# Attention scores from float32r halves of queries and keys, moved to their rows by DMA, and GraphSAGE's bias product over 128 rows

## The chip, the cores and the metric

The kernel runs on one core of one Trainium2 chip, in one launch. The core has five engines that run side by side, each in the order of its own program: TensorE (PE, with its weight loads shown as PEld), VectorE (DVE), ScalarE (ACT), GpSimd (POOL) and SyncE (SP), which here only issues transfers. They meet through semaphores. Sixteen DMA engines carry the transfers that SP, ACT and POOL issue. The metric is the device time of one execution in microseconds (us).

## The reference

Two graph layers over 16 graphs of 1024 nodes with 128 features. Each layer normalises its input, applies ReLU, computes, and adds the result to its input.

```python
# layer 0: attention over the edges, 8 heads of 16
h = relu(layernorm(x))
q, k, v = h @ Wq.T + bq, h @ Wk.T + bk, h @ Wv.T + bv        # split into heads
scores = q @ k.T / sqrt(16);  scores[adj == 0] = -inf
attn = softmax(scores) * adj;  attn = attn / (attn.sum(-1) + 1e-8)
x = x + (attn @ v) @ Wo.T + bo
# layer 1: dilated neighbours, then three GraphSAGE layers
h = relu(layernorm(x));  adj_d = adj * dilate(adj > 0)         # row by row, sequential
for i in 1..3:
    out = (adj_d @ h / max(sum(adj_d), 1)) @ Wr_i + h @ Wx_i + b_i
    h = h_i = batchnorm(relu(out / norm(out)))
x = x + concat(h_1, h_2, h_3) @ Wl + bl
```

`dilate` walks the 1024 rows of each graph and removes every n-th neighbour of a row, in both directions; it needs the adjacency alone.

## The kernel before

**First stage: attention, with the dilation beside it.** The attention loop (`attention`, L471) runs over 256 turns `(b, c, m)`: graph b, half c of the 512 query nodes, tile m of 128 key nodes. A turn has two half-turns, one for each head group g: heads 2j + g, j = 0 to 3. In a half-turn

- `scores` (L530) puts -1e30 where there is no edge, with sixteen small bf16 products over 32x32 strips (L545), and adds the scores with four products (L551), one head each, on the four 32-row strips of the array;
- ScalarE takes exponentials in two pieces of 1024 columns (L589), VectorE multiplies each by the transposed adjacency tile `aT` (L594);
- PE adds the values product and the 1e-8 term of the half-turn before (`values`, L475, lines L478 and L483).

The query and key projections give 128 rows, 16 to a head, so each 32-row strip holds two neighbouring heads, one of either group. `key` (L311) writes them to SBUF as they are (`kT`, L316). `query` (L302) writes two copies (L307), in each of which the rows of the other group are multiplied by zero through the column `own`. So a product over 32 rows gives one head's scores. Operands are float32.

`turn_over` (L488), two turns ahead, transposes the adjacency tile on PE (L496), stores it to HBM as `aT_d` for the second stage (L500), makes the no-edge mask, and has SP shift that mask to other partitions with six transfers (L507, L508). `load` fetches adjacency tiles three turns ahead.

Everything else of the attention, the preparation of the next graph (`prepare`, L284: layer norm, transposes, key, value and query projections of either half) and the conclusion of the last one (`conclude`, L379: division, output projection, layer norm for the next layer), is written as generators. The loop takes one step of them at fixed places of a half-turn (`go_on_with`, L461): "True" steps, which need a PSUM bank, in the second half-turn of a turn, and "evict" steps, which empty that bank, after the exponentials and multiplications of the same half-turn.

The dilation (`dilation`, L642) is VectorE work, with ScalarE and PE helping. It goes through 8 blocks of 128 rows, for all graphs at once: seven counting rounds in small steps (L829 and the lines around), then a sweep over the 16 graphs' whole rows (L892 to L924), which stores removed edges to HBM (`mr_d`). `beside_attention` (L935) feeds its steps in after each half-turn, in proportion to planned costs, so that the dilation ends just before the attention does. The sweep's row tiles `wr` and `er` have rings of their own; the rounds use a ring of four buffers named `mr`.

**Second stage: GraphSAGE.** Three layers, 16 graphs, two halves: 96 turns. A turn (`nodes`, L1091) begins with the bias, a product of a 3-row matrix of ones with the bias split into three bf16 pieces (`start_with`, L108, L111), adds the node's own term (L1102), sums the neighbours in four groups of products (L1116), and ends in normalisation on VectorE. `edges` (L128) loads 2 MB of adjacency (L132) and two mask tiles (L136) for a turn, three turns ahead, into buffers `aT0` to `aT3`; the third of these buffers holds the attention's value rows `v1_both` until the attention is over. VectorE applies the masks (L145). Between the stages the conclusion of the last half graph runs inside the first GraphSAGE turns.

**Order.** In both stages the programs of PE, ScalarE and VectorE run in the order in which the Python code emits them. SP and POOL also issue in order: an issue that waits for its data holds back those behind it.

Of the kernel before, what the change touches and what calls it, by code (L numbers as in the profile page):

```python
# [10 lines left out]
F32 = mybir.dt.float32  # L11
BF = mybir.dt.bfloat16
# [9 lines left out]
P = 128  # L22
# [12 lines left out]
def swept(ctx: ExitStack, tc: tile.TileContext, t: dict, out: bass.AP, flag: bass.AP):  # L35
# [11 lines left out]
    H = 8  # L47
# [34 lines left out]

    ones3 = const.tile([3, P], BF, name="ones3")
    nc.vector.memset(ones3, 1.0)
# [3 lines left out]
    bias3 = const.tile([3, len(names), D], BF, name="bias3")  # L88
# [19 lines left out]
    def start_with(ps_tile, pieces):  # L108

        n = ps_tile.shape[1]  # L110
        nc.tensor.matmul(  # L111
            ps_tile.rearrange("p k d -> p (k d)"), ones3, pieces.unsqueeze(1).to_broadcast([3, n, D]),
            start=True, stop=False,
        )
# [51 lines left out]
    def first_part(p1):  # L166
# [33 lines left out]
        raw = pool.tile([P, 4, D], F32, name="raw", tag="kT")  # L200
        for i, name in enumerate(names):
# [3 lines left out]
        bk = one.tile([P, 1], F32, name="bk")  # L205
        nc.sync.dma_start(bk, t["L0_gnn_bk"].rearrange("(d o) -> d o", o=1))

        own = one.tile([P, 2], F32, name="own")
        nc.vector.tensor_reduce(
            own,  # L210
            ident.rearrange("p (j g d) -> p g j d", g=2, d=HD),
            AX.XY,
            ALU.add,
        )
        bq = one.tile([P, 3], F32, name="bq")
        nc.sync.dma_start(bq[:, 2:3], t["L0_gnn_bq"].rearrange("(d o) -> d o", o=1))
# [3 lines left out]
        def turn_weights():  # L220
            wps = ps_d.tile([P, 4, D], F32, name="wps", tag="d")
            for i in range(4):
                nc.tensor.transpose(wps[:, i, :], raw[:, i, :], ident)
            yield
            nc.vector.tensor_copy(attn_w, wps)
            nc.vector.tensor_tensor(bq[:, 0:2], own, bq[:, 2:3].to_broadcast([P, 2]), ALU.mult)
            yield
# [13 lines left out]
        v1_both = shared.tile([P, 2, NB, H, 32], F32, name="v1_both", tag="aT2")  # L241
        v1s = [v1_both[:, i] for i in range(2)]
        for v1 in v1s:
            nc.vector.memset(v1[:, :, :, HD:], 0.0)
            nc.vector.memset(v1[:, :, :, HD : HD + 1], 1.0)
# [38 lines left out]
        def prepare(b):  # L284
# [15 lines left out]
            kT = pool.tile([P, N], F32, name=f"kT_{b}", tag="kT")  # L300

            def query(c, bank=(ps_m, "m")):  # L302
# [3 lines left out]
                for g in range(2):  # L306
                    nc.scalar.activation(  # L307
                        qTs[c][:, g, :], pq, AF.Identity, bias=bq[:, g : g + 1], scale=own[:, g : g + 1]
                    )

            def key(c, bank=(ps_m, "m")):  # L311
# [4 lines left out]
                nc.scalar.activation(kT[:, cc], pk, AF.Identity, bias=bk)  # L316
# [3 lines left out]
            def value(c, bank=(ps_m, "m")):  # L320
                pv = bank[0].tile([P, HB, D], F32, name=f"pv_{b}_{c}", tag=bank[1])
                start_with(pv, bias3[:, 0, :])
                for i in range(HB):
# [6 lines left out]
                    v1[:, c * HB : (c + 1) * HB, :, :HD], pv.rearrange("p k (h d) -> p k h d", d=HD)  # L330
                )

            if b == 0:
# [14 lines left out]
                qTs = [pool.tile([P, 2, HN], F32, name=f"qT_{b}_0", tag="qT")]  # L348
                yield from query(0, (ps_d, "d"))
                yield from second  # L350
                ready[b] = (xt, qTs, kT, v1)
# [3 lines left out]
                yield from turned(1)  # L355
            else:
# [7 lines left out]

                yield "half 1"
                qTs = [pool.tile([P, 2, HN], F32, name=f"qT_{b}_0", tag="qT")]
                yield True
                yield from query(0)

            ready[b] = (xt, qTs, kT, v1)  # L370
            for what in (key, value):
                yield True
                yield from what(1)
            yield "half 0"
            qTs.append(pool.tile([P, 2, HN], F32, name=f"qT_{b}_1", tag="qT"))
            yield True
            yield from query(1)

        def conclude(b, c, acc, xt):  # L379

            yield False
            cx = small.tile([P, HB, H, HD], F32, name=f"cx_{b}_{c}", tag="cx", bufs=1)
# [30 lines left out]
            start_with(pr, bias3[:, 1, :])  # L413
# [31 lines left out]
        ready = {}  # L445

# [24 lines left out]
        def attention():  # L471
# [3 lines left out]
            def values(acc, v1, m, g, es, ws):  # L475

                for j in range(4):
                    nc.tensor.matmul(  # L478
                        acc[g][32 * j : 32 * j + 32, :], v1[:, m, 2 * j + g, :],
                        ws[j // 2][:, j % 2, :], start=(m == 0), stop=False,  # L480
                    )
# [48 lines left out]
            def scores(i, g):  # L530
# [4 lines left out]
                _, qTs, kT, _ = ready[b]  # L535
                nomask = tiles[i][1]
                mm = slice(m * P, (m + 1) * P)
# [11 lines left out]
                for j in range(4):  # L549
                    rows = slice(32 * j, 32 * j + 32)  # L550
                    nc.tensor.matmul(  # L551
                        scs[j // 2][:, j % 2, :], kT[rows, mm], qTs[c][rows, g, :],
                        start=False, stop=True, tile_position=(32 * j, 0),
                    )
# [3 lines left out]
            for i, (b, c, m) in enumerate(turns):  # L558
# [12 lines left out]
                for g in range(2):  # L571
# [32 lines left out]
                    go_on_with(False)  # L604
                    if i + g + 1 < len(turns):
# [36 lines left out]
        def dilation():  # L642
# [84 lines left out]
            for k in range(NB):  # L727
# [151 lines left out]
                wrs, gms, ers, ets = {}, {}, {}, {}  # L879
# [8 lines left out]
                for i in range(B + 2):  # L888
                    b = i
                    if b < B:  # L890
                        wrs[b] = pool.tile([P, N], F16, name=f"wr_{k}_{b}", tag="wr", bufs=2)
# [15 lines left out]
                    if 0 <= b < B:  # L907
                        er = ers[b] = pool.tile([P, N], BF, name=f"er_{k}_{b}", tag="er", bufs=3)
# [56 lines left out]
        def judge():  # L965
# [5 lines left out]
            fits = pool.tile([P, B * NB * H], F32, name="fits", tag="kT")  # L971
# [119 lines left out]
    def nodes(L, b, c, hT, aT):  # L1091
# [7 lines left out]
        start_with(own, bias3[:, 2 + L, :])  # L1099
# [859 lines left out]
```

## Time and profile before

| | |
|---|---|
| median of 3 runs | 3486.12 us (3484.86 to 3486.22) |
| the profiled execution | 3484.92 us |
| its span, first to last instruction | 3483.0 us |
| PE busy | 3389.0 us (97%) |
| VectorE busy | 3092.4 us (89%) |
| ScalarE busy | 2286.4 us (66%) |
| GpSimd busy | 174.4 us (5%) |
| last exponentials of the attention | 2353.6 us after the start |

Lines such as L551 are those of the kernel before. A group's row gives line, engine, operation, what it writes and reads, shape and number, then its busy time, the mean time of one in nanoseconds, and the idle time of the engine just before its instructions with what ended it. Busy time counts overlapping instructions once: four products that run together on four strips of the array are busy for as long as one, although each has its own mean. Matmul ends are modelled. In a table by stretches of time the columns are busy us (and instructions) of PE, PEld, DVE, ACT and POOL, the granted PE clock, the DMA share and GB/s.

### The profile page before, as it was taken

To read this page: it belongs to the slowest core of one execution; us is meant where nothing else is said; L and a number is where in the kernel's file an instruction comes from. 1 tells how busy PE (TensorE), PEld (TensorE's weight loads), DVE (VectorE), ACT (ScalarE), POOL (GpSimd) and SP (SyncE) were. 2 spreads that over 40 slices of the span, in tenths; PEclk is the share of its full clock that TensorE was granted. 3 is DMA by queue.
4 is the path that set the end of the run, shared out by engine and by line. 5 is a ranking of instruction groups with operands and counts; after the bars stand their busy time and mean duration, and the time that the engine had idled before them with its cause. 6 is when DMAs were issued, how large, how long until landed. Compare 5 with 4: busy or idle time off the path is not lost. (4 is left out here: it accounts for less than half of the span.)

```text
span 3483.0 us, 86073 instructions
## 1 busy us (share of the span) xinstructions
PE 3389.0 (97%) x34855; PEld 1877.8 (54%) x34855; DVE 3092.4 (89%) x5254; ACT 2286.4 (66%) x3781; POOL 174.4 (5%) x253
## 2 busy tenths in 40 slices
PE   8999999999999999999999999999999899999997
PEld 3333333333333333333333334338999899989997
DVE  7899999989989989999999998988788788878886
ACT  7699689789779869868977886873222333332224
POOL 2000000000000000000000000000000000000000
PEclk9999999999999999999999999999999999999999
DMA  7366456447547647736754864768999799989996
GB/s 239 108 175 197 131 158 195 150 140 218 171 130 219 190 125 208 231 113 186 229 157 141 243 199 128 218 190 314 330 333 325 270 328 326 335 309 332 332 333 215
DMA packets 650121, 772.27 MB, mean 222 GB/s; under 512 B 173264, under 2 KB 569168, under 8 KB 637424
## 3 DMA queue, kind: packets, MB, share of 16 engines
q1 hardware_dynamic: 632672, 708.58, 63.1%
q0 software_dynamic: 15456, 57.30, 5.0%
q8 instruction: 275, 4.51, 0.6%
q14 instruction: 134, 1.10, 0.1%
q10 hardware_dynamic: 1584, 0.79, 0.1%
HBM read 508.50 MB, written 157.29 MB: 191 GB/s over the span
## 5 line engine op out<-in xcount | busy, mean ns | idle before, releaser
L594 DVE TENSOR_TENSOR w<-e,aT 128x1024 f32<-128x1024 f32 x1024 | 1203.6, 1216 | 104.0 <-ACT e L589 103.4
L589 ACT ACTIVATE e<-sc 128x1024 f32<-128x1024 f32 x1024 | 990.5, 1020 | 341.9 <-PE sc L551 340.8
L1116 PE MATMUL pg<-y,aT 128*128 128x128 f32 (+1 forms) x6144 | 737.3, 275 | 0.0
L1116 PEld LDWEIGHTS pg<-y,aT 128*128 128x128 f32 x6144 | 711.7, 192 | 0.0
L478 PE MATMUL acc<-w,v_both 128*32 128x512 f32 x4096 | 636.4, 605 | 8.0 <-DVE w L594 4.9
L483 PE MATMUL acc<-e,eps 128*32 128x512 f32 x4096 | 617.2, 593 | 0.0
L551 PE MATMUL sc<-qT,kT 32*128 32x512 f32 x4096 | 584.0, 640 | 0.5 <-ACT qT L307 0.5
L145 DVE SCALAR_TENSOR_TENSOR aT<-mr,aT 128x1024 f32<-128x1024 bf16 x384 | 458.7, 1216 | 0.0
L483 PEld LDWEIGHTS acc<-e,eps 128*32 128x32 f32 x4096 | 159.0, 110 | 293.8 <-issue 284.9
L1139 ACT ACTIVATE sq<-o 128x512 f32<-128x512 f32 x96 | 60.6, 631 | 361.6 <-DVE o L1134 361.6
L892 DVE TENSOR_TENSOR_SCAN wr<-rk 128x1024 f16<-128x1024 bf16 x128 | 291.6, 2278 | 0.0
L545 PEld LDWEIGHTS <-never 32*32 32x32 bf16 x8192 | 78.4, 88 | 339.3 <-issue 317.3
L545 PE MATMUL sc<-nomask,never 32*32 32x512 bf16 x8192 | 246.5, 385 | 11.8 <-ACT e L589 6.7
L551 PEld LDWEIGHTS sc<-qT,kT 32*128 32x128 f32 x4096 | 160.0, 183 | 116.9 <-issue 116.1
L478 PEld LDWEIGHTS acc<-w,v_both 128*32 128x32 f32 x4096 | 100.6, 108 | 204.7 <-DVE w L594 105.8
L496 PEld LDWEIGHTS pa<-ident,a 128*128 128x128 f32 x1024 | 107.8, 141 | 181.6 <-issue 139.7
L1157 ACT COPY hT<-pt 128x512 f32<-128x512 f32 x96 | 56.2, 585 | 224.2 <-PE pt L1153 214.3
L1134 DVE SCALAR_TENSOR_TENSOR o<-pg,rdeg,mine 128x128 f32<-128x128 f32 x384 | 108.1, 344 | 88.9 <-PE pg L1116 87.1
L905 ACT ACTIVATE wr<-wr,th 128x1024 f16<-128x1024 f16 x128 | 148.0, 1156 | 46.7 <-DVE wr L892 45.7
L496 PE MATMUL pa<-ident,a 128*128 128x128 f32 x1024 | 168.4, 287 | 6.9 <-DMA a<-in_adj 6.2
L503 ACT ACTIVATE nomask<-aT 128x512 bf16<-128x512 f32 x256 | 161.3, 630 | 8.1
L499 ACT COPY aT<-pa 128x512 f32<-128x512 f32 x256 | 151.6, 592 | 5.3 <-PE pa L496 4.8
(225 smaller groups left out, 3840.7 us busy)
## 6 DMA issues: line engine op xcount, KB each, us to landing
aT<-aT_d SPq DMA_DIRECT2D x94, 2048.0 KB, 9.1
mr<-mr_d SPq DMA_DIRECT2D x188, 512.0 KB, 5.9
aT_d<-aT SPq DMA_DIRECT2D x256, 256.0 KB, 4.2
a<-in_adj SPq DMA_DIRECT2D x253, 256.0 KB, 4.1
ad<-in_adj SPq DMA_DIRECT2D x112, 512.0 KB, 4.2
nomask<-nomask SPq DMA_DIRECT2D x512, 96.0 KB, 2.7
nomask<-nomask SPq DMA_DIRECT2D x512, 64.0 KB, 2.7
nomask<-nomask SPq DMA_DIRECT2D x512, 32.0 KB, 2.8
```

Source lines behind the costliest of these rows:

```text
L145: nc.vector.scalar_tensor_tensor(part, mrs[h][:, j : j + 2, :].rearrange("p j n -> p (j n)"), 0.0, part, ALU.is_equal, ALU.mult)
L478: nc.tensor.matmul(acc[g][32 * j : 32 * j + 32, :], v1[:, m, 2 * j + g, :], ws[j // 2][:, j % 2, :], start=(m == 0), stop=False,)
L483: nc.tensor.matmul(acc[g][32 * j : 32 * j + 32, :], eps8, es[j // 2][:, j % 2, :], start=False, stop=(m == NB - 1),)
L496: nc.tensor.transpose(pa[:, k * P : (k + 1) * P], a[:, k, :], ident)
L499: nc.scalar.copy(aT[:, 0, :], pa)
L503: nc.scalar.activation(nomask[:, 0, :], aT[:, 0, :], AF.Relu, bias=1.0, scale=-1e38, accum_out=zeros[:, i : i + 1])
L545: nc.tensor.matmul(scs[j // 2][to : to + 32, j % 2, :], never[rows, rows], nomask[rows, j, :], start=True, stop=False, tile_position=(32 * ...
L551: nc.tensor.matmul(scs[j // 2][:, j % 2, :], kT[rows, mm], qTs[c][rows, g, :], start=False, stop=True, tile_position=(32 * j, 0),)
L589: nc.scalar.activation(e, scs[q], AF.Exp, scale=1.0 / math.sqrt(HD))
L594: nc.vector.tensor_tensor(w, es[q], aT.to_broadcast([P, 2, HN]), ALU.mult)
L892: nc.vector.tensor_tensor_scan(wrs[b], rk(b, 1, N + 1), rk(b, 2, N + 2), -1023.0, ALU.add, ALU.add)
L1116: nc.tensor.matmul(pg[:, i // 2, at : at + width], aT[:, j, i * P : (i + 1) * P], y[:, j, :width], start=(j == 0), stop=(j == NB - 1),)
```

## The change

**Scores.** A float32 score product becomes two float32r products. `halves` splits a projection as it leaves PSUM: ScalarE adds the bias and writes the result rounded to float32r, and VectorE writes what is left (product plus bias minus the rounded value), also as float32r. Both go to one buffer, `split_home`. The projection weights are turned with their columns in another order, so that heads of group 0 come first: head j of group g stands in rows 16(4g + j) on.

`move` then queues sixteen transfers from there to a tile that `scores` reads. Strip j has 32 rows: 16 for one half of the head's key, 16 for the other (`ks`, a tile for each half of the nodes, with one copy for each g). In the queries' tile (`qs`) both 16-row parts of a strip hold the same rows, once for each of the two halves. A product over 32 rows gives (key's first half + key's second half) times one half of the query; `scores` runs two of them, one for each half of the query, in groups of four strips. Transfers of group 0 go through POOL's queue, those of group 1 through SP's. `move_on(8)` at the end of a half-turn issues up to eight of those that are queued; for the first graph's first key and query `move_on(16)` issues all at once before the attention loop starts.

**Room.** The value rows take 17 columns a head instead of 32 in the same 16 KB (`both`), which now also holds `cx` of `conclude` and `split_home`. The sweep's `wr` and `er` become pairs in the `mr` ring. The biases of query and key come in with sixteen small loads. In graphs past the first the second half's value comes before its key.

**Bias.** The matrix of ones and the bias pieces have 128 rows, those past the third zero; GraphSAGE's products run over all 128, the attention's over three as before.

```diff
-    ones3 = const.tile([3, P], BF, name="ones3")
+    ones_bf = const.tile([P, P], BF, name="ones_bf")
...
-    bias3 = const.tile([3, len(names), D], BF, name="bias3")
+    bias3 = const.tile([P, len(names), D], BF, name="bias3")
+    nc.vector.memset(bias3, 0.0)
...
-    def start_with(ps_tile, pieces):
+    def start_with(ps_tile, i, rows=3):
         n = ps_tile.shape[1]
         nc.tensor.matmul(
-            ps_tile.rearrange("p k d -> p (k d)"), ones3, pieces.unsqueeze(1).to_broadcast([3, n, D]),
+            ps_tile.rearrange("p k d -> p (k d)"), ones_bf[:rows], bias3[:rows, i, :].unsqueeze(1).to_broadcast([rows, n, D]),
             start=True, stop=False,
         )
...
+        bqk = one.tile([P, 2], F32, name="bqk")
+        for i, name in enumerate(("L0_gnn_bq", "L0_gnn_bk")):
+            by_g = t[name].rearrange("(j g d o) -> g j d o", g=2, d=HD, o=1)
+            for g in range(2):
+                for j in range(4):
+                    at = (4 * g + j) * HD
+                    nc.sync.dma_start(bqk[at : at + HD, i : i + 1], by_g[g, j])
...
-        v1_both = shared.tile([P, 2, NB, H, 32], F32, name="v1_both", tag="aT2")
+        HW = HD + 1
+        VW = H * HW + 16
+        both = shared.tile([P, 4096], F32, name="both", tag="aT2")
...
+        cx_home = both[:, free : free + HN]
+        split_home = both[:, free + HN : free + 3 * HN].rearrange("p (t n) -> p t n", t=2)
+        split_r = split_home.bitcast(F32R)
...
+            def halves(ps_tile, bias):
+                nc.scalar.activation(split_r[:, 0, :], ps_tile, AF.Identity, bias=bias)
+                nc.vector.scalar_tensor_tensor(
+                    split_r[:, 1, :], ps_tile, bias, split_home[:, 0, :], ALU.add, ALU.subtract
+                )
+
+            def move(dst, piece):
+                assert not moves
+                for n in range(16):
+                    g, j, i = n % 2, n // 4, n // 2 % 2
+                    here, there = (4 * g + j) * HD, 32 * j + HD * i
+                    moves.append(partial(
+                        (nc.gpsimd, nc.sync)[g].dma_start,
+                        dst[there : there + HD, g].bitcast(F32), piece(split_home[here : here + HD], i),
+                    ))
...
                 yield "evict"
-                for g in range(2):
-                    nc.scalar.activation(
-                        qTs[c][:, g, :], pq, AF.Identity, bias=bq[:, g : g + 1], scale=own[:, g : g + 1]
-                    )
+                halves(pq, bq)
+                qs.append(pool.tile([P, 2, 2, HN], F32R, name=f"q_{b}_{c}", tag="qM"))
+                move(qs[c], lambda rows, i: rows)
...
-                nc.scalar.activation(kT[:, cc], pk, AF.Identity, bias=bk)
+                halves(pk, bk)
+                ks.append(pool.tile([P, 2, HN], F32R, name=f"k_{b}_{c}", tag="kA", bufs=3))
+                move(ks[c], lambda rows, i: rows[:, i])
...
                 yield from key(0)
-                qTs = [pool.tile([P, 2, HN], F32, name=f"qT_{b}_0", tag="qT")]
+                move_on(16)
                 yield from query(0, (ps_d, "d"))
+                move_on(16)
...
-                for j in range(4):
-                    rows = slice(32 * j, 32 * j + 32)
-                    nc.tensor.matmul(
-                        scs[j // 2][:, j % 2, :], kT[rows, mm], qTs[c][rows, g, :],
-                        start=False, stop=True, tile_position=(32 * j, 0),
-                    )
+                for half in range(2):
+                    for j in range(4):
+                        rows = slice(32 * j, 32 * j + 32)
+                        nc.tensor.matmul(
+                            scs[j // 2][:, j % 2, :], ks[m // HB][rows, g, mm], qs[c][rows, g, half, :],
+                            start=False, stop=(half == 1), tile_position=(32 * j, 0),
+                        )
...
                     go_on_with(False)
+                    move_on(8)
...
-                        wrs[b] = pool.tile([P, N], F16, name=f"wr_{k}_{b}", tag="wr", bufs=2)
+                        pairs[b] = shared.tile([P, 2, N], BF, name=f"pair_{k}_{b}", tag="mr", bufs=4)
+                        wrs[b] = pairs[b][:, 0, :].bitcast(F16)
...
-                        er = ers[b] = pool.tile([P, N], BF, name=f"er_{k}_{b}", tag="er", bufs=3)
+                        er = ers[b] = pairs.pop(b)[:, 1, :]
...
-        start_with(own, bias3[:, 2 + L, :])
+        start_with(own, 2 + L, P)
```

## The prediction

> **What bounds the kernel now.** I read the busy table by stage first. Columns: length, then busy us (instructions) of PE, PEld, DVE, ACT, POOL, the PE clock, the DMA share, GB/s.
>
> ```profile
> 0.00:20.00 20.00, 10.85 (x48) 4.95 (x48) 9.86 (x43) 9.23 (x18) 10.06 (x26) 1.00 0.75 218
> 20.00:2356.00 2336.00, 2305.55 (x25738) 846.62 (x25736) 2173.84 (x3371) 1906.68 (x2986) 118.08 (x141) 1.00 0.59 177
> 2356.00:3483.00 1127.00, 1072.61 (x9071) 1026.27 (x9071) 908.71 (x1842) 370.45 (x779) 46.24 (x86) 0.99 0.88 315
> ```
>
> Attention with dilation ends near 2356. In it PE is busy 98.7%, VectorE 93.1%, ScalarE 81.6%: PE is first, VectorE close behind. GraphSAGE is PE's too (95%). Cutting the first stage where the dilation changes its kind of step (its counting rounds, then its row sweeps) splits this:
>
> ```profile
> 1028.00:1178.00 150.00, 147.99 (x1552) 54.22 (x1548) 145.73 (x214) 142.43 (x238) 6.06 (x6) 1.00 0.75 215
> 1178.00:1321.00 143.00, 140.67 (x1644) 51.23 (x1647) 129.38 (x212) 101.21 (x153) 6.85 (x8) 1.00 0.44 133
> ```
>
> The row sweeps (first) leave VectorE 4.3 us idle in 150, the rounds 13.6 in 143. Only the rounds have room. The groups, busy and mean:
>
> ```profile
> L594 DVE TENSOR_TENSOR w<-e,aT 128x1024 f32<-128x1024 f32 x1024 | 1203.6, 1216 | 104.0 <-ACT e L589 103.4
> L551 PE MATMUL sc<-qT,kT 32*128 32x512 f32 x4096 | 584.0, 640 | 0.5 <-ACT qT L307 0.5
> L545 PE MATMUL sc<-nomask,never 32*32 32x512 bf16 x8192 | 246.5, 385 | 11.8 <-ACT e L589 6.7 <-DMA nomask<-nomask 3.5 <-DMA a<-in_adj 0.5
> L314 PE MATMUL pk<-hT,attn_w 128*128 128x512 f32 x64 | 36.9, 659 | 0.7 <-ACT aT L499 0.7
> L420 DVE TENSOR_TENSOR xt<-xt,pr 128x512 f32<-128x512 f32 x32 | 21.5, 672 | 10.0 <-PE pr L415 10.0
> ```
>
> There are 512 half-turns (256 key tiles, two head groups). Scores take 584.0/512 = 1.14 us of PE in each. A float32 product leaves two records: 32 key products gave 64, 36.9/32 = 1.15 us each. So one pass is 0.57 us. VectorE's largest wait, 103.4 us, is for the exponentials, which themselves wait for scores (340.8 us of ScalarE): this is what faster scores can give back.
>
> **What the Trainium skill says.** "TensorE: Matmul & The Clock Gate", Part 3, says products on different 32-row strips run together. The trace agrees: four strip products take 1.14 us, one full-array product 1.15. "TensorEngine Tiling (Array Packing)", Key Properties, says a change of tiling mode drains the array; the three-row bias product fits that (below). "SBUF — State Buffer", two separate sides, says VectorE can lock GpSimd out of its port while it writes DMA descriptors. GpSimd's 128x8 power takes 2.0 to 2.7 us against 1.04 for 128x4 at the start, while VectorE's 1024-column product stays within 1192 to 1227 ns: I expect late POOL transfers, not a slower VectorE. No page prices float32r.
>
> **The change, part by part.**
>
> *Scores.* Two passes of one float32 product become two float32r products over the same rows. Unknown. Low: the TensorE page's warm gap (Back-to-back issue gap), 512 columns in 216 ns, so 0.43 us a half-turn. High: each streams like a float32 pass, 1.14, no gain. I take 0.30 each, 0.60: bf16 streaming plus part of the overhead that the float32 pass shows. PE sheds 512 x 0.54 = 276 us, leaving 2305.6 - 276 = 2029. PE is then no bound.
>
> *Halves.* 64 evictions gain one VectorE instruction from PSUM; nearest row L420, 0.67 us: 43 us, 62 of them (41.5) in the body. ScalarE has 32 fewer 128x512 activations: some 22 us less, in slack.
>
> *The body.* VectorE's work becomes 2173.8 + 41.5 = 2215. In the sweeps above it runs at 145.73/150 = 97.1% although PE is at 98.7%; with PE freed I take 97% everywhere: 2284, that is -52. At 99%: 2238 (-98). At 95%: 2332 (-4).
>
> *Moves in the body.* 62 x 16 transfers, eight issued at the end of each of two half-turns, four a queue. SP's shifts cost 0.59 us each, POOL's issues 0.54: 2.4 and 2.2 us of a 4.56 us half-turn. They wait for VectorE's half, and behind them on SP stand the next adjacency load, the aT_d store and six shifts; on POOL the layer norm's power and the rden copy. The load is used a turn (9.1 us) later and lands in 4.1; shifts have a turn more. The single split_home must be drained before the next eviction, two half-turns on. Zero, covered by these turns; uncovered, up to 1 us of ScalarE each, 62 us (a rival). Data is 48 MB on a stage whose DMA share is 0.59: hidden. The pairs in the mr ring are reused four sweep steps later, some 9 us after their stores (3 to 4 us): hidden.
>
> *The start.* Serial, because the attention loop starts after it:
>
> ```profile
> 15.70 1.85 PE L304 MATMUL pq<-hT,attn_w 128*128 128x512 f32 x2
> 17.59 1.45 ACT L307 ACTIVATE qT<-pq,bq,own 128x512 f32<-128x512 f32 x2 [0.95 <-PE pq L304]
> 18.42 1.14 PE L551 MATMUL sc<-qT,kT 32*128 32x512 f32 x8 [0.51 <-ACT qT L307]
> 18.51 0.59 SPq L508 DMA_DIRECT2D nomask<-nomask  x1
> ```
>
> SP is busy with shifts to 19.1; sixteen small bias loads for two (0.33 to 0.43 each) push that to about 22. Eight key moves: 22 + 8 x 0.59 = 26.7, landing 2.7 later at 29.4 (POOL's eight from 17.3 end near 28). Only then may the query be split: 30.8. Its moves: SP 35.5, landed 38.2; POOL 30.8 + 4.3 + about 6 (its other transfers land in 6 to 7) = 41. First scores at 41 instead of 18.4: +22; +10 if issues and landings are half that, +30 at worst.
>
> *GraphSAGE's bias product*, 96 times on PE's path:
>
> ```profile
> L111 PE MATMUL own<-bias,ones 3*128 3x512 bf16 x96 | 37.2, 387 | 0.0
> L1102 PEld LDWEIGHTS own<-weights,h 128*128 128x128 f32 x768 | 93.5, 192 | 22.0 <-issue 22.0
> ```
>
> The next weight load stands idle 22.0/96 = 0.23 us behind each. At 128 rows nothing need drain and 0.216 us of streaming hides that load: between 0 and 0.23 saved, I take 0.15: -14 (0 to -22). The three-row products of attention stay.
>
> *At nothing:* the values' rows of 17 instead of 32 columns (the product still loads 32), three weight copies for one (0.69 us, beside SP's backlog), smaller memsets, the key after the value in batches past the first (it has until the fifth key tile of the next batch).
>
> *The hand-over.* Context rows now live in the tile of the values, which GraphSAGE's third adjacency tile takes over:
>
> ```profile
> 2358.32 0.33 SPq L132 DMA_DIRECT2D aT<-aT_d  x1
> 2365.71 0.60 PE L405 MATMUL pc<-ident,cx 128*128 128x128 f32 x4
> 2378.08 1.21 DVE L145 SCALAR_TENSOR_TENSOR aT<-mr,aT 128x1024 f32<-128x1024 bf16 x1
> ```
>
> The load moves from 2358.3 to after the transposes, 2366.3, and with 9.1 us lands at 2375.4, before its first reader. Two mask loads queue behind it. 0 to +8; I take +2.
>
> Sum: -52 + 22 - 14 + 2 = -42. The profiled execution took 3484.92 us (span 3483.0), the median is 3486.12, 1.2 above: 3486 - 42 = 3444.
>
> **Rivals.**
>
> *VectorE near full* (13%). If 99% is reached and the start costs 12: 3486 - 98 + 12 - 18 = 3382 to about 3400. For it: most of VectorE's listed waits are for scores. Against: its work per half-turn is uneven, and the values product of one half-turn, which waits for VectorE, stands ahead of the next scores on PE.
>
> *The moves are not hidden* (18%). Evictions find split_home undrained: up to 62 x 1 us on ScalarE and on VectorE behind it: 3444 + 20 to 62, 3465 to 3506. For it: POOL's slow descriptors, and ScalarE 95% busy in the sweeps. Against: half a turn of cover.
>
> *float32r is no faster than a float32 pass* (14%). PE keeps its 2305, takes back nothing, and VectorE's 41 us are hidden only in the rounds: about +25 of them, +22 start, -14: 3486 + 25 + 22 - 14 + 2 = 3521, slower. On a straight line between the forecast's body (-52 at 0.30 us a half product) and this one (+25 at 0.57) the sum is zero near 0.45 us; above that the change is slower. For it: both read four-byte elements. Against: two records per float32 product say that the extra passes are what is removed.
>
> *The bias product saves nothing* (7%, else the forecast): 3444 + 14 = 3458. For it: GraphSAGE's DMA share is 0.88, next behind PE. Against: no PE wait there is put down to a DMA.
>
> **How the numbers follow.** The forecast (3444, own range 3415 to 3472) has 48%, the rivals 13, 18, 14 and 7. Range 3400 to 3510: below it lies half of the first rival (6), above it most of the third (12). No change means within 0.2%, 3479 to 3493, about what three runs of this kernel can tell. The moves rival splits into 4 faster, 8 same, 6 slower. Faster: 48 + 13 + 7 + 4 = 72; same 8; slower 14 + 6 = 20.
>
> **What would show it.** Right: scores near 0.6 us of PE a half-turn; PE below 92% of the first stage and VectorE near 97%; first scores near 41; a bias product whose follower waits no longer. Wrong: scores still near 1.1; ScalarE waiting ahead of the splits; VectorE at 93% or less with PE idle, which would mean that the order of work, not an engine, sets the pace.

## The result and the profile after

The changed kernel takes **3675.2 us** (median of 4 runs, 3672.4 to 3687.0) where the kernel before takes 3486.2 beside it: a ratio of **1.0549**, interval 1.0526 to 1.0573. The forecast was 3444, its range ended at 3510. The change is 189 us slower.

The profiled execution has a span of 3671.5 us. Busy time by stage, in the columns used before:

```profile
0.00:43.00 43.00, 15.11 (x44) 6.14 (x44) 9.98 (x46) 9.16 (x18) 17.81 (x42) 1.00 0.77 191
43.00:2536.00 2493.00, 2220.89 (x25634) 868.01 (x25629) 2211.98 (x3425) 1884.08 (x2944) 361.26 (x637) 0.95 0.65 184
2536.00:3671.00 1135.00, 1063.80 (x9183) 1036.50 (x9183) 917.28 (x1849) 379.33 (x787) 46.30 (x86) 0.98 0.87 313
```

The middle row is the finding. PE's work has become less (2221 us instead of 2306, though the forecast had 2029) and VectorE's is 2212 us as worked out (2215), but the stage has become 157 us longer as the table divides it, and no engine is full: PE 89%, VectorE 89%, ScalarE 76%. The groups of instructions that answer to those shown before:

```profile
L631 DVE TENSOR_TENSOR w<-e,aT 128x1024 f32<-128x1024 f32 x1024 | 1204.1, 1217 | 157.0 <-ACT e L626 155.2
L588 PE MATMUL sc<-q,k 32*128 32x512 f32 x4096 | 408.4, 448 | 64.2 <-DMA q<-both 63.6 <-issue 0.2
L532 PE MATMUL pa<-ident,a 128*128 128x128 f32 x1024 | 178.8, 301 | 194.1 <-DVE both L314 120.1 <-DMA a<-in_adj 59.6 <-ACT e L626 11.5
L314 DVE SCALAR_TENSOR_TENSOR both<-pk,bqk,both 128x512 fp32r<-128x512 f32 x32 | 23.8, 744 | 2.4 <-ACT both L313 2.4
L313 ACT ACTIVATE both<-pq,bqk 128x512 fp32r<-128x512 f32 x32 | 22.1, 690 | 103.1 <-DMA k<-both 98.0 <-PE sc L588 2.6 <-DVE w L631 1.3
```

Scores cost PE 408.4/512 = 0.80 us a half-turn instead of 1.14. What is new stands behind the last bar. PE's transposes of the adjacency (`pa`), which waited 6.9 us before, wait 194; the line of the kernel before is

```profile
L496 PE MATMUL pa<-ident,a 128*128 128x128 f32 x1024 | 168.4, 287 | 6.9 <-DMA a<-in_adj 6.2 <-ACT hT L297 0.7
```

In the changed kernel ScalarE's split of a query waits 98 us for the moves of the key before it; the scores wait 64 us for moved queries. VectorE, which does most of the work, waits 155 us for exponentials (103 before). The waits themselves, with number and longest:

```profile
DVE w L631 <- ACT e L626: 155.2, 103, 13.1
PE pa L532 <- DVE both L314: 120.1, 48, 11.7
ACT both L313 <- DMA k<-both: 98.0, 15, 12.3
PE sc L588 <- DMA q<-both: 63.6, 32, 14.6
PE pa L532 <- DMA a<-in_adj: 59.6, 21, 6.3
```

One such place in order of time (start, duration, then what was waited for in brackets), in a graph that runs beside a row sweep:

```profile
1434.90 2.44 SPq L481 DMA_DIRECT2D k<-both  x4
...
1440.15 1.56 SPq L189 DMA_DIRECT2D a<-in_adj  x1
...
1443.02 0.38 SPq L536 DMA_DIRECT2D aT_d<-aT  x1
...
1447.27 2.49 SPq L481 DMA_DIRECT2D k<-both  x4
...
1450.78 0.69 ACT L313 ACTIVATE both<-pq,bqk 128x512 fp32r<-128x512 f32 x1 [11.80 <-DMA k<-both]
...
1451.50 0.75 DVE L314 SCALAR_TENSOR_TENSOR both<-pq,bqk,both 128x512 fp32r<-128x512 f32 x1 [9.35 <-ACT both L313]
1452.31 0.71 PEld L532 LDWEIGHTS pa<-ident,a 128*128 128x128 f32 x4 [12.16 <-DVE both L314]
```

SP's second four moves of the key, issued one half-turn after the first by the code, start 12.4 us after them: in front stand the sweep's stores, the next adjacency load, the store of `aT_d` and six shifts. The query may not be split until these moves have drained `split_home`; the query's PSUM bank is not free until it is split; the next transposes need that bank. ScalarE, VectorE and PE stop one behind the other for some 12 us. "TensorE: Matmul & The Clock Gate", Part 1, of the Trainium skill says that an idle window of about 3.4 us brings the TensorE clock down; the records agree in part. PE has 24 gaps over 3 us in this stage (none before), and its granted clock is 0.95 where it was 1.00; but without moves (experiment 2) no gap between the first and the last exponentials is over 3 us, and the clock is still at 0.99. What the clock costs was not measured by itself, but it is a small part of the loss at most: between the first and the last exponentials PE is busy 2229 us here and 2192 without moves, and it stands idle 11% of the stage.

Between the first and the last exponentials lie 2333 us before and 2501 after; the first come at 43.2 us instead of 20.5; from the last to the end it is 1129.4 before and 1127.5 after. So +22.7 (start), +168 (body), -2 (GraphSAGE), together the 188.5 us between the spans. (The table above ends the stage 8 us before the last exponentials, so that it shows 157 for the body.)

### The profile page after: what moved, and what is told of

Read it like the earlier page. It is cut to its first block, busy times and chain, and to the rows that moved or that the text cites. A ratio compares the mean times of both kernels' runs of the same rounds, so it can differ in the third digit from the quotient of the medians.

```text
span 3671.5 us, 88289 instructions
## 1 busy us (share of the span) xinstructions
PE 3299.8 (90%) x34855; PEld 1910.7 (52%) x34855; DVE 3139.2 (86%) x5319; ACT 2272.6 (62%) x3749; POOL 425.4 (12%) x765
## 4 chain that ended last, share of the span: by engine, by line
PE 35%; DVE 33%; DMA 11%; ACT 9%; SPq 6%; issue 4%; POOL 0%; ACTq 0%; DVEq 0%; POOLq 0%
DVE w L631 13%; PE pg L1155 13%; PE acc L514 4%; DMA nomask<-nomask 4%; ACT e L626 4%; PE acc L519 3%; DVE aT L147 3%; DVE pair L931 3%; PE sc L588 3%; SPq L544 2%; PE pn L1126 2%; SPq L543 2%; DMA a<-in_adj 2%; DVE o L1173 2%; PE pt L1192 2%
## 5 line engine op out<-in xcount | busy, mean ns | idle before, releaser
L631 DVE TENSOR_TENSOR w<-e,aT 128x1024 f32<-128x1024 f32 x1024 | 1204.1, 1217 | 157.0 <-ACT e L626 155.2
L514 PE MATMUL acc<-w,both 128*32 128x512 f32 x4096 | 679.7, 641 | 13.3 <-DVE w L631 10.3
L519 PE MATMUL acc<-e,eps 128*32 128x512 f32 x4096 | 651.4, 622 | 0.0
L588 PE MATMUL sc<-q,k 32*128 32x512 f32 x4096 | 408.4, 448 | 64.2 <-DMA q<-both 63.6
L147 DVE SCALAR_TENSOR_TENSOR aT<-mr,aT 128x1024 f32<-128x1024 bf16 x384 | 458.8, 1217 | 0.0
L532 PE MATMUL pa<-ident,a 128*128 128x128 f32 x1024 | 178.8, 301 | 194.1 <-DVE both L314 120.1
L931 DVE TENSOR_TENSOR_SCAN pair<-rk 128x1024 f16<-128x1024 bf16 x128 | 291.6, 2278 | 0.0
L588 PEld LDWEIGHTS sc<-q,k 32*128 32x128 f32 x4096 | 169.8, 184 | 194.5 <-issue 136.0
L514 PEld LDWEIGHTS acc<-w,both 128*32 128x32 f32 x4096 | 101.2, 110 | 226.5 <-DVE w L631 133.1
L481 POOL DMA_DIRECT2D k<-both x256 | 123.3, 488 | 564.9 <-ACT both L313 544.0
L481 POOL DMA_DIRECT2D q<-both x256 | 123.3, 488 | 383.7 <-DVE both L314 160.1
L944 ACT ACTIVATE pair<-pair,th 128x1024 f16<-128x1024 f16 x128 | 147.9, 1155 | 32.1 <-DVE pair L931 31.6
```

What stands on the lines that cost most here:

```text
L147: nc.vector.scalar_tensor_tensor(part, mrs[h][:, j : j + 2, :].rearrange("p j n -> p (j n)"), 0.0, part, ALU.is_equal, ALU.mult)
L481: moves.pop(0)()
L514: nc.tensor.matmul(acc[g][32 * j : 32 * j + 32, :], v1[:, m, (2 * j + g) * HW : (2 * j + g) * HW + 32], ws[j // 2][:, j % 2, :], start=(m ...
L519: nc.tensor.matmul(acc[g][32 * j : 32 * j + 32, :], eps8, es[j // 2][:, j % 2, :], start=False, stop=(m == NB - 1),)
L532: nc.tensor.transpose(pa[:, k * P : (k + 1) * P], a[:, k, :], ident)
L588: nc.tensor.matmul(scs[j // 2][:, j % 2, :], ks[m // HB][rows, g, mm], qs[c][rows, g, half, :], start=False, stop=(half == 1), tile_positi ...
```

## The experiments

All changes are against the changed kernel unless "before" is named. Ratios are to the kernel before on the same chip. Experiments 2, 5 and 6 carry the argument: without the moves, with moves that nobody reads on either queue, and with moves that are read on either queue. `split_home`, the buffer in which the halves lie until they are moved, is called their home.

**1. The bias product alone.** The kernel before with bias operands of 128 rows.

```diff
-            start_with(own, bias3[:, 2 + L, :])
+            start_with(own, 2 + L, P)
```

> The kernel before with the bias product over 128 rows and nothing else. As forecast, 0.15 us a GraphSAGE turn on the path of PE: 3486 - 14 = 3472. The trace of the changed kernel says otherwise: layer 0 keeps its 9.93 and 10.82 us a turn, and in the later two only every second turn is shorter, 11.37 for 11.67 us. By that, 2 x 16 x 0.3 = 9.6 us: 3476. If the product is hidden everywhere: 3486.

3479.8 us, ratio 0.9978 (0.9969 to 0.9987). GraphSAGE, from the last exponentials on, takes 1121.6 us instead of 1129.4. It is a gain of 7.8 us, about half of the forecast's 14. The idle time ahead of the next weight load did go, as forecast (22.0 us to 3.9, here in the changed kernel):

```profile
L1141 PEld LDWEIGHTS own<-weights,h 128*128 128x128 f32 x768 | 103.5, 196 | 3.9
```

But layer 0's turns stay at 9.9 and 10.8 us, and in layers 1 and 2 only every second turn gets shorter (11.67 to 11.37): the saving counts in a third of the 96 turns.

**2. No moves.** The halves are written straight to the tiles that `scores` reads, and nothing is moved. The products then take rows that do not belong together; the work of every engine is that of the changed kernel.

```diff
-                halves(pq, bq)
-                qs.append(pool.tile([P, 2, 2, HN], F32R, name=f"q_{b}_{c}", tag="qM"))
-                move(qs[c], lambda rows, i: rows)
+                qs.append(pool.tile([P, 2, HN], F32R, name=f"q_{b}_{c}", tag="qM"))
+                halves(pq, bq, qs[c])
```

> The changed kernel without its moves: the same ScalarE and VectorE instructions write the two halves straight into the tiles that the scores read, and a head group's copies are left out, so the scores are wrong sums; every instruction of PE, ScalarE and VectorE is kept. If the moves (their queues and the waits for them) are the cause, the forecast comes true without its start: 3486 - 52 + 3 - 10 = 3427, at most 3450. If the cause is on the engines (float32r products, more work on VectorE, a lower PE clock by itself), it stays above 3600.

3477.1 us, ratio 0.9975 (0.9963 to 0.9986): far below 3600, so the engines' own work is not the cause; the 3427 to 3450 expected without moves was too low. So the moves cost 198 us, more than the whole loss. Without them the stage reads (length, then the columns as above):

```profile
20.00:2346.00 2326.00, 2198.04 (x25760) 853.53 (x25759) 2213.72 (x3434) 1887.79 (x2956) 119.54 (x141) 0.99 0.60 178
```

VectorE is the fullest engine now, at 2213.72/2326 = 95.2%, or 2211.5/2316.9 = 95.5% between the first and last exponentials. The forecast took 97%. Everything but the moves gives 8.7 us by the ratio, not 42.

**3. Which of the changed kernel's waits is it?** Four runs relieve one thing each: all moves on POOL's queue; the next graph's half-1 key before its value, as half 0 has it; sixteen moves at one step instead of eight; a second home for keys (the tile of the normalised input, which is free by then).

```diff
-                        (nc.gpsimd, nc.sync)[g].dma_start,
+                        nc.gpsimd.dma_start,
```

> All sixteen moves of a projection on POOL's queue, none on SP's. If SP's queue is the bound (it issues for 40 of 50 us in the row sweeps even before), this gives back most of the loss: 3440 to 3500, with the start still about 20 us late. If the single buffer for the halves is the cause (an eviction waits until the moves of the last one are through), sixteen issues of 0.48 us on one queue take as long as before: 3620 to 3680. If POOL's slow descriptors are the cause: slower than 3675.

3663.1 us, ratio 1.0508 (1.0490 to 1.0526). PE's wait for the adjacency tile falls from 60 to 7.8 us, but the waits for queries rise to 86.9 us and ScalarE still waits 69 for the home: SP was not all of it.

```diff
-                for what in (value, key):
+                for what in (key, value):
```

> The changed kernel with the second half's key ahead of its value again, so that the value's turn stands between the key's moves and the query's eviction. If the wait of the query's eviction for the key's moves is the cause (98 us of ScalarE, 120 us of PE behind it): 3560 to 3590. If SP's queue is short of issue time whatever the order: 3650 to 3680.

3716.0 us, ratio 1.0654 (1.0632 to 1.0675): slower than the change itself. PE's wait for the half in PSUM grows from 120 to 183 us, and ScalarE's wait is now mostly for the query's moves (106 us).

```diff
-                    move_on(8)
+                    move_on(16)
```

> The changed kernel with all sixteen moves of a projection issued at the end of the half-turn that made them. If the loss is that SP's last four stand behind the next turn's load, store and six shifts (8 us late in the trace) while the first scores of a graph and the second query's eviction wait for them: 3540 to 3590. If SP has too little issue time for all of them: 3650 to 3700, since the shifts now come later.

3664.0 us, ratio 1.0509 (1.0491 to 1.0526). The waits for the home fall from 98 to 43 us and for queries from 64 to 26, but PE's wait for the adjacency tile, whose load stands behind the moves on SP, rises from 60 to 127.

```diff
-                halves(pk, bk)
+                home = h_home if b > 0 or c == 1 else split_home
+                halves(pk, bk, home)
```

> The changed kernel with keys split into a buffer of their own (the normalised input, which is free by then; the first key excepted), so a query's eviction never waits for a key's moves. If that wait is half of the loss: 3560 to 3590, with PE's waits for the queries left. If the query's late moves only pass the wait on to the scores, or SP is short of time: 3650 to 3680.

3653.2 us, ratio 1.0485 (1.0463 to 1.0507). The wait for the home is gone but for one at the start (12.4 us), and that for the adjacency tile is 118 us. Each relief uncovered the next wait. Two homes and sixteen at once together:

> Two edits of earlier runs together: keys split in a home of their own, and all sixteen moves issued at one step. The sums are those of the changed kernel. If the loss is the sum of independent waits for the moves (home 98 us, first query 64 us), both are shortened here and the time falls by most of them, to 3530 or less. If the moves cost through SP's crowded queue, where the adjacency loads stand behind them, the waits for the adjacency tile stay above 100 us and the time stays at 3620 to 3660.

3670.6 us, ratio 1.0534 (1.0512 to 1.0556): no gain that can be told. The wait for the adjacency tile is 144 us, so the sum of independent waits is ruled out.

**4. SP's load by itself, first try.** The kernel before with eight small SP transfers between idle tiles for each projection.

```diff
                 nc.scalar.activation(kT[:, cc], pk, AF.Identity, bias=bk)
+                move(32)
```

> The kernel before, with eight more 16-row transfers of 128 bytes a row on SP's queue for each of the 64 projections, four at the end of each of two half-turns, between two tiles that nothing else uses. If SP's issue time is what is short (40 of 50 us in the row sweeps, these add some 5 us a projection): 3560 to 3650. If the loss comes from who waits for the moves, not from their number: 3486 to 3500.

3739.2 us, ratio 1.0721 (1.0703 to 1.0739), above both expectations, but it does not say what it was made for. The transfers depend on nothing, and SP did not issue them where the code names them: the last of the 512 went out 566 us after the start, up to nineteen in a row.

```profile
68.75 11.96 SPq L462 DMA_DIRECT2D idle_dst<-idle_src  x19
80.82 0.53 SPq L187 DMA_DIRECT2D a<-in_adj  x1
```

In the first two graphs a turn takes about 16 us (9 in the kernel before), and SP issues in 44 to 46 of every 50: here the queue sets the pace by issues of 0.6 us alone. After it nothing is slower. The idle load of the next experiment depends on something that keeps it in its place.

**5. The load without the waiting.** Experiment 2 again (its scores leave the same products out), with the sixteen moves of each projection copying the halves to a tile that nobody reads. They are held in place by the halves; no engine waits for one. Once on both queues as in the change, once on POOL's.

```diff
+                idle = pool.tile([P, 2, 2, HN], F32R, name=f"iq_{b}_{c}", tag="iM", bufs=1)
+                move(idle, lambda rows, i: rows, qs[c])
```

> The kernel with the halves written straight to their tiles, and beside that the same sixteen moves for each projection on the same two queues at the same steps, copying the halves to a tile that nobody reads: the load without anybody waiting for a move. The scores lack the products between rows that the moves would bring together, so the sums are wrong. Theory 'waits for the moves': near the kernel without moves, 3477 to 3510. Theory 'SP's crowded queue' (adjacency loads and shifts behind the moves): 3580 to 3660.

3659.4 us, ratio 1.0475 (1.0443 to 1.0506). Without a reader the moves cost 182 of their 198 us. The other 16 are no more than the later start: the first exponentials come at 25.1 us here and at 43.2 in the change, and from the first to the last it is 2510 us here and 2501 there. So the long waits for moves in the change do not come on top of SP's load; where nobody waits for a move, the reader of the adjacency load pays about as much.

> The same idle moves, all sixteen on POOL's queue, eight a step; scores as in the run before it leave products out. Theory 'waits for the moves' and theory 'SP's crowded queue' both say 3477 to 3500, as nobody waits and SP is free of them. If the traffic of the moves itself, or POOL's delayed work, cost something, it is above 3520.

3543.2 us, ratio 1.0145 (1.0119 to 1.0170): 66 us over the kernel without moves (59 by the ratios), as only the last case of the expectation had it, traffic or POOL's delayed work. Half of the moves on SP, as in the run before, cost 116 us more (by the intervals, known to some 14 us). The waits of the first run, which has nearly all of the loss:

```profile
PE pa L534 <- DMA a<-in_adj: 162.2, 37, 11.8
DVE w L633 <- ACT e L628: 135.7, 98, 9.5
```

and of the second, on POOL:

```profile
PE pa L534 <- DMA a<-in_adj: 5.8, 1, 5.8
DVE w L633 <- ACT e L628: 94.0, 82, 9.4
```

The adjacency wait, 162 us on both queues, is 5.8 on POOL (6.2 in the kernel before, 5.9 without moves). One of the 37, in order of time:

```profile
622.22 3.55 SPq L483 DMA_DIRECT2D ik<-k  x4
625.87 0.53 SPq L965 DMA_DIRECT2D mr_d<-et  x1
...
628.45 0.44 SPq L189 DMA_DIRECT2D a<-in_adj  x1
...
634.81 1.09 PE L534 MATMUL pa<-ident,a 128*128 128x128 f32 x4 [7.28 <-DMA a<-in_adj]
```

From 617.9 to 628.4 SP issues without a pause: `aT_d`, six shifts, four moves, five transfers of the dilation. The load goes out when they are done, lands some 6 us later, and PE has stood for 7.3 us by then. What is late is the issue and not the transfer: from issue to landing the adjacency loads take 4.0 us (median) here, 4.2 with all moves on POOL and 4.1 in the kernel before. Nor does SP stand waiting for the halves: all waits ahead of its 512 moves sum to 30 us.

**6. Moves on POOL that are read.** Two homes, sixteen at one step, all on POOL: SP's load, the home and the slow issue are relieved together.

> All sixteen moves at one step, all on POOL's queue, keys split in a home of their own. The sums are those of the changed kernel. Theory: the loss is waits for the moves (single home, first query of a graph) and SP's crowding, and nothing else; all are relieved together here, so the time falls to 3480 to 3540, near the kernel without moves (3477). Rival: POOL's queue holds the moves behind its own waits for VectorE, or the traffic itself costs; then the waits for keys and queries stay and the time is above 3600.

3625.2 us, ratio 1.0388 (1.0370 to 1.0405). Above the 3600 of the rival, and 82 us more than the idle moves on POOL. One wait holds it:

```profile
PE sc L592 <- DMA q<-both: 88.6, 40, 14.4
```

The time of two turns, from the starts of VectorE's products (mean over graphs 1 to 14, us; a graph is eight such pairs), says where:

| pair of turns | 1 | 2 | 3 | 4 | 5 | 6 | 7 | 8 |
|---|---|---|---|---|---|---|---|---|
| no moves | 20.1 | 18.5 | 18.4 | 19.1 | 18.0 | 17.2 | 17.5 | 17.3 |
| the change | 27.7 | 18.5 | 19.4 | 19.4 | 18.2 | 17.5 | 17.1 | 19.8 |
| idle moves, both queues | 21.5 | 23.7 | 20.3 | 19.4 | 18.0 | 17.4 | 17.2 | 20.0 |
| idle moves, POOL | 21.3 | 19.2 | 18.5 | 19.1 | 18.0 | 17.3 | 17.5 | 18.7 |
| read, POOL, two homes | 22.1 | 18.5 | 18.4 | 19.1 | 18.0 | 17.2 | 17.1 | 24.4 |
| the same, query early | 20.9 | 19.1 | 18.4 | 19.1 | 18.0 | 17.3 | 17.5 | 18.9 |

The last pair holds 7 us: the next graph's first query leaves PSUM some 12 us, little more than a turn, before its first reader, and its sixteen moves are not there. The last row makes that query before the first values instead of after them, two half-turns earlier:

```diff
-                for what in (key, value):
-                    yield True
-                    yield from what(0)
-                yield "half 1"
-                yield True
-                yield from query(0)
+                yield True
+                yield from key(0)
+                yield "half 1"
+                for what in (query, value):
+                    yield True
+                    yield from what(0)
```

> All sixteen moves at one step on POOL's queue, two homes, and the next graph's first query made before its first values instead of after them (two half-turns earlier). The sums are those of the changed kernel. In the run without the early query the last two turns of a graph take 24.4 us instead of 17.3 and the wait for the moved query is 89 us; with it 15 graph changes lose about 7 us each. Theory: distance of the first query is that loss, so the time falls by about 105 us to 3515 to 3545, near the idle moves on POOL (3543). Rival: the wait only moves to the keys or to POOL's queue, and the time stays above 3590.

3546.8 us, ratio 1.0182 (1.0163 to 1.0200), 78 us less (72 by the ratios, 105 were expected), and the wait for queries falls to 17.1, of which 13.6 stand at the start. It stands where the idle moves on POOL stand (3543), so the readers' waiting is gone. The same order with the moves on both queues:

> The same order and two homes, sixteen moves at one step, but on POOL and SP as in the changed kernel. The sums are those of the changed kernel. Theory 'SP's crowded queue': the waits for the moves are relieved, those for the adjacency tile behind the moves stay, and the time stays at 3620 to 3670 like the idle moves on two queues (3659). Rival 'waits for the moves alone': as fast as the run on POOL, below 3560.

3660.6 us, ratio 1.0509 (1.0491 to 1.0526), where the idle moves on both queues stand (3659), with an adjacency wait of 122.5 us. The four runs form a square: SP or POOL makes 114 to 116 us, read or not read 1 to 4, which is within the noise. (The two kernels that read their moves start 17 to 20 us later, at 44 to 45 us, and are 15 to 25 us shorter from there; they also issue sixteen at a step, so the small difference is a net one.)

**7. PE's relief without halves.** The kernel before with q and k rounded once to float32r and one product. It leaves out the second halves, so its scores are those of rounded operands; nothing is split, moved or copied.

```diff
-            kT = pool.tile([P, N], F32, name=f"kT_{b}", tag="kT")
+            kT = pool.tile([P, N], F32R, name=f"kT_{b}", tag="kT")
```

> The kernel before with keys and queries rounded to float32r as they are written, and one float32r product in place of the float32 one (so the scores are rounded): PE sheds some 0.75 us a half-turn and VectorE gets no extra work. If VectorE then runs at the 95.5 per cent that the kernel without moves shows: 2173.8 / 0.955 = 2276 for the body of 2336, so 3486 - 60 = 3426. If it runs at 97 per cent, as forecast: 3486 - 95 = 3391. If the order of the work sets the pace: above 3460.

3419.8 us, ratio 0.9811 (0.9795 to 0.9828). VectorE's work is that of the kernel before, its share again 2167.53/2270 = 95.5%:

```profile
20.00:2290.00 2270.00, 2150.56 (x23684) 812.36 (x23688) 2167.53 (x3369) 1901.73 (x2982) 118.95 (x141) 0.99 0.61 182
```

Faster scores are worth some 66 us. The kernel without moves is 57 us slower than this one: 62 more VectorE instructions of 0.745 us at 95.5% make 48 of them, a start 7.7 us later the rest, as its wider bias and its hand-over about cancel.

> The kernel before with q and k rounded once to float32r and one product (no halves, no moves), and the bias product over 128 rows. The scores are those of rounded q and k, not exact ones. The two edits alone gave 3419.8 and 0.9978 of before; if they add, 3410 to 3415; if the start of GraphSAGE is hidden otherwise, 3420.

3417.0 us, ratio 0.9803 (0.9786 to 0.9819): the lowest time of the study, faster than both kernels, but not told apart from the run before it. GraphSAGE took 1122.0 us (1129.9 without the wider bias), the attention 5 us longer. It trades accuracy of the scores for time; of the versions that keep float32 scores the wider bias alone, 3480, is the best seen.

## Why the prediction was wrong

**The step that failed is "Moves in the body", priced at zero.** The moves cost 198 us. The step set their own issue time (2.4 us on SP) against a half-turn of 4.56 us and called the rest cover. It named what stands behind them on SP, but not how full that queue was: summed from the timeline of the kernel before, SP's issues take 36 to 42 of 50 us well inside the row sweeps. In a turn of about 9.5 us that leaves 1.5 to 2.7 us, and the eight SP moves of a projection, 4.7 us, come twice within two turns where half 1's key and query follow each other. Its cover for the load, "used a turn (9.1 us) later and lands in 4.1", counted a load that starts on time. Shown: with half of them on SP instead of all on POOL the same idle transfers cost 116 us more, and the adjacency wait goes from 5.8 to 162; 66 us stay with all of them on POOL, and 16 are the start. What the prediction gave as the sign of its being wrong, VectorE at 93% or less with PE idle and ScalarE waiting ahead of the splits, is what the profile has.

**The rival "the moves are not hidden" had the sign and a wrong size.** It allowed 62 waits of up to 1 us on ScalarE. The home did make ScalarE wait, 15 times for 98 us, 6.5 each. But taking the home's wait away gave 22 us, and taking it away with the slow issue 5: behind it SP's queue held the same turns. A bound by one waiting engine was no bound, since VectorE and PE, the PSUM bank and the adjacency load stood behind it in a row.

**"The body", VectorE 97% everywhere: too high.** Without moves it is 95.5%, both with the halves (2212 us of work) and without (2168). At 95.5% the step's own formula gives 2215/0.955 = 2319 and -17 instead of -52; measured -16 (2333 to 2317). The 97.1% had been read in a row sweep. Without moves the first of the two stretches that the prediction shows, a sweep, has 146.39/150 = 97.6%, and the second, of counting rounds, 136.92/143 = 95.7%: a share read where side work fills the gaps does not hold for the whole stage.

**"Scores", 0.60 a half-turn: 0.74** (379.5/512 without moves), so the scores shed 204 us, not 276. PE's busy time fell by less still, from 2306 to 2198, because the values' products grew. These are the lines without moves:

```profile
L512 PE MATMUL acc<-w,both 128*32 128x512 f32 x4096 | 705.6, 615 | 27.5 <-DVE w L629 21.2
L517 PE MATMUL acc<-e,eps 128*32 128x512 f32 x4096 | 676.8, 603 | 0.0
L586 PE MATMUL sc<-q,k 32*128 32x512 f32 x4096 | 379.5, 444 | 0.0
```

In the kernel before the first two were busy 636.4 and 617.2 us, with nearly the same time of one (605 and 593 ns). Eight products of each kind belong to a half-turn. From the first start to the last end the median group of the first kind takes 1.07 us in both kernels, but 37% of the groups take more than 1.3 us, against 24% before: in the timeline these start in parts, with a wait for VectorE's second piece between, and fewer of them run side by side. "PE is then no bound" is therefore not shown: without moves it is busy 94.5% of the stage, VectorE 95.2%, and what the miss cost stays open. **"Halves"**, 0.67 an instruction: 0.745; the sum of VectorE's work was right within 3 us.

**"The start", +22: right, +22.7.** In order of time:

```profile
23.68 4.96 SPq L481 DMA_DIRECT2D k<-both  x8
...
29.60 0.69 ACT L313 ACTIVATE both<-pq,bqk 128x512 fp32r<-128x512 f32 x1 [12.32 <-DMA k<-both]
...
31.10 5.87 SPq L481 DMA_DIRECT2D q<-both  x8
```

Key moves, drained home, split query, query moves: the chain is the one worked out, within a few us at each point. Here the queue was followed issue by issue; in the body it was not. Not all of the 22.7 is the moves': without them the first exponentials already come at 27.4 us, because PE waits for shifts that SP issues late.

**"GraphSAGE's bias product", -14: -7.8**, inside its bounds; the 0.23 us of idle goes, but only a third of the turns gets shorter. **"The hand-over", +2: about +6** (GraphSAGE is 1127.5 us long in the change, 1121.6 with the bias alone), inside its 0 to 8; the third turn takes 15.7 us instead of 11.2. The other runs that have it lie between 1120.8 and 1130.0.

**"Late POOL transfers, not a slower VectorE": right**, though the line that it rested on compared 128x8 with 128x4, twice the elements. In the change moves land in 2.5 (keys) and 4.1 us (queries) from POOL and in 2.1 and 2.9 from SP (medians), and VectorE's product stays at 1217 ns.

**What stays open.** Sixteen moves a projection on POOL still cost 66 us though nobody waits for them (3543 against 3477). Transfers land later (shifts 3.2 instead of 2.7 us, adjacency 4.2 instead of 3.7, medians). The scores wait 29.8 us for the shifts (7.6 without moves). More falls on VectorE itself, which waits for two loads of the dilation:

```profile
DVE rk L747 <- DMA gl<-mr_d: 27.6, 10, 6.8
DVE rk L725 <- DMA ad<-in_adj: 19.2, 4, 11.9
```

Without moves these are 6.5 and 2.4 us. Whether one of these waits is the cause was not tried.

## What to carry to other kernels

Before putting transfers on a queue, sum what that queue already issues in the stretch concerned, stage by stage, and place the new issues in its order. In this kernel the added issues were paid by the adjacency load behind them, whose reader had no slack left, and by the engines behind that reader. "DMA: Bandwidth & Descriptors", Rules for kernel authors, of the Trainium skill says that spreading transfers over several issuers only saves issue time. Most of the loss here was of that kind, and it was not small: 116 us for 512 issues on SP. When relieving a wait leaves the time where it was, run the load without its readers, and the readers without the load, before believing in any single wait.

## What the runs showed that was not expected

- Where a small transfer is issued mattered more than what it carries: 512 of the 1024 transfers cost 116 us more on SP than on POOL, and all of them on POOL 66, while the DMA share of the stage rose only from 0.59 to 0.65 in the change and to 0.70 with idle moves on POOL, the faster of the two.
- Two float32r products over a half-turn (eight records) take 0.74 us of PE where two passes of float32 take 1.14; a single one (four records) is 259.3/512 = 0.51. The second one adds 0.23.
- VectorE's share of the stage was 95.5% with 2168 us of its work and with 2212, although PE was busy 2150 us in the one kernel and 2192 in the other: the larger relief of PE did not raise it.
